# Where kept tiles are sent from, which row sums VectorE adds, and how the last attention ends: one change to a two-layer graph kernel

## The chip, the cores and the metric

The kernel runs on one core of one Trainium2 chip. A core has TensorE (PE: matrix products into PSUM, and loads of the stationary operand, PEld), VectorE (DVE), ScalarE (ACT), GpSimd (POOL) and SyncE (SP), which run side by side, each in the order of its own instruction list, and wait for each other by semaphores. Data between the chip's memory (DRAM below) and the on-chip buffers is moved by DMA engines, to which SP, ACT and POOL hand transfers. The metric is device time of one execution in microseconds (us), lower is better. Everything is computed in 32-bit floats.

## The reference, cut to what matters

Input is x (4096 nodes, 512 features) and a 0/1 adjacency adj (4096 x 4096). Two layers with a residual follow each other. Layer 0 is an auto-encoder with four attention heads that uses one attention twice, layer 1 a usual graph attention with four heads of 128 features:

```python
h = jnp.maximum(_layernorm(x), 0.0)
# layer 0: encoder attention, batch norm, MLP, decoder attention (same att), MLP
Xw  = jnp.einsum('hnd,hde->hne', Xh, W)
sig = jax.nn.sigmoid(f1[:, :, None] + f2[:, None, :])
att = masked_softmax(sig, adj)                       # per head, 4096 x 4096
Xn  = _batchnorm(jnp.einsum('hij,hjd->hid', att, Xw))
emb = _mlp_block(Xn)                                 # elu(x W + b) + x, batch norm
Y   = jnp.einsum('hij,hjd->hid', att, emb)           # then W, elu, _mlp_block
x   = x + out
# layer 1: graph attention
h = jnp.maximum(_layernorm(x), 0.0)
logits = leaky_relu(e_s[:, :, None] + e_n[:, None, :], 0.2) masked by adj
x = x + relu(softmax(logits) @ feats + b)
```

So three large attentions are computed: the encoder's, the decoder's (same weights as the encoder's, other values) and the graph attention's. In each, a weight tile is made from a row of target scores and a column of source scores, masked, and multiplied with the values; the row sums of the weights are the denominators of the softmax.

## The kernel before, in words

All three attentions go through one function, `attention` (L221). It works on eight blocks, four heads times two halves of 2048 targets. A block has 32 steps j, one for each 128 source nodes. A step makes one weight tile `e` (128 x 2048) and then four matmuls of 128 x 512 (L371, and L368 for the fourth bank of the first steps) add its products to four PSUM banks.

- **Encoder** (kept="write"). ScalarE makes tanh (L450) and exp (L451), VectorE multiplies by the mask (L452). The mask of a step is loaded by SP (L210, 256 KB as bytes, five buffers); the target row of the next block is loaded by SP too (L203, 1 MB). Every fifth weight tile (j % 5 == 4) is kept for the decoder: ScalarE's queue stores it to DRAM (`ekeep`, L358, 1 MB), three steps later in the program, and the last of a block in the next block (L412) or, in the last block, at its end (L410). `weight_tile` (L249) hands out eight buffers here.
- **Decoder** (kept="read"). The same, without row sums, and every fifth tile is loaded by SP from `ekeep` (L343).
- **Graph attention.** ScalarE makes a Relu with scale and bias (L905), VectorE adds a column and multiplies by the mask (L906). Nine buffers.

Row sums in encoder and graph attention are collected in three ways, and the plans at L62 to L69 say which step goes which way: "moved" tiles are added up by accumulating DMAs that POOL issues (L386), steps "by ones" go to a PSUM bank `den` by four narrow matmuls with ones (`add_to_den`, L259), and the rest VectorE adds to a tile `acc` (L392, L394). At a block's end `acc` goes through the ones matmuls as well; with a third entry True in the plan (`ends_later`), the sum of the moved tiles follows in step 1 of the next block.

In all blocks but the last, the results stay in SBUF or PSUM and are finished within the next block, by a list of things due at step numbers (`at`, L290, and `ending`, L294): copy out of PSUM, denominators through DRAM, inverse, spread over the partitions, multiplication, and what follows. The last block of graph attention finishes at once (L421 to L442): the last two steps' products are made after the row sums (`late`, L376 and L423), VectorE adds a small number to the sums and inverts them (L434, L435), four matmuls with the identity spread the inverses over the partitions (L440), and per 512 targets ScalarE adds the self term (`out_gat`, L911), VectorE multiplies (L915), ScalarE adds the bias with Relu (L918), VectorE adds the residual (L921) and SP writes the result (L922). The encoder's last block takes the same way with one late step.

The order on each engine is that of a scheduler over the program, with `pinned` and `tc.issue_after` as orders written by hand. Every engine works its list in order, so a store in ScalarE's list that waits for a tile holds up the activations behind it.

Of the kernel before, what the change touches and what calls it, by code (L numbers as in the profile page):

```python
# [31 lines left out]
FP = mybir.dt.float32  # L32
# [39 lines left out]

# [13 lines left out]
def kernel(ctx, tc, x, xT, adjT, w0, w0T, v0, wencT, wdecT, vecs, w1, w1T, a1, outT):  # L86
# [132 lines left out]


    def attention(what, keep, pools, weights, values, row_of, out, finish, ebufs, modes=None, invert=None,  # L221
                  kept=None, sums=None, sums2=None, extras={}, row0=None, masks0=(), in_parts0=1):

# [97 lines left out]
        for n, (h, tb) in enumerate(blocks):  # L321
# [7 lines left out]
            adds, held, stores, next_row = [], [], [], None  # L329
            for j in range(NJ):  # L330

                with pinned(products_of):
# [9 lines left out]
                if store and kept == "read":  # L342
                    a_load = nc.sync.dma_start(e, ekeep[h][tb][j // KEEP])  # L343
                else:
                    if masks0:
                        a, a_load = masks0.pop(0)
                    else:
                        a = mask_tile(keep)
                        a_load = load_mask(a, tb, j)

                    with pinned(products_of[:1] if kept == "read" and n == 0 and j < 8 else []):
                        products_of = weights(e, rowb, a, j, h, SB if NJ * n + j < in_parts0 else 1)
                    if store:
                        stores.append((j // KEEP, e))

                    if j % KEEP == KEEP - 3 and stores:
                        k, t = stores.pop()
                        nc.scalar.dma_start(ekeep[h][tb][k], t)  # L358

                def products():  # L360
                    nonlocal last_main, last_ones
# [11 lines left out]
                    last_ones = None  # L373


                if last and invert is not None and j >= NJ - (1 if kept is not None else 2):  # L376
                    late.append((j, e))
                else:
                    products()
                if j < EVICT:  # L380
                    ahead.append((j, e))
                if invert is not None:
                    if j in moved:

# [36 lines left out]
            for s, b in enumerate(po):  # L421
                for k, t in late:
                    nc.tensor.matmul(b, block(values[h], k), t[:, s * IB:(s + 1) * IB], start=(k == 0),  # L423
                                     stop=(k == NJ - 1))
# [10 lines left out]
            nc.vector.reciprocal(inv, inv)  # L435
            if kept is not None:
                nc.gpsimd.dma_start(rinvs[h][tb].rearrange("o (s i) -> (o s) i", i=IB), inv[0:P:32, :])
            for s, o in enumerate(outs):
                rb = bank()
                nc.tensor.matmul(rb, ident[:, 32 * s:32 * s + 1].to_broadcast([P, P]), inv, start=True, stop=True)  # L440
                for f in finish:
                    f(spool, h, tb, s, o, rb, True)  # L442
# [14 lines left out]
    with tc.tile_pool(name="keep", bufs=1) as keep:  # L457
# [149 lines left out]
        def mlp_block(work, w, src, dst, gamma, beta, scale, between, early=None):  # L607
# [11 lines left out]
            for o in range(C):  # L619
# [7 lines left out]
                for ib in range(NIB):  # L627
# [16 lines left out]
                    nc.vector.bn_stats(stats[:, o, ib, :], d)  # L644
                    between(o, ib)
                bn_coefs(stats, gamma, beta, a_mlp, b_mlp, o, o + 1)
            return last_product

        with tc.tile_pool(name="m_small", bufs=1) as small, tc.tile_pool(name="m_work", bufs=3) as work:
# [7 lines left out]
            mlp_block(work, w, xc, yc, "enc_mlp_bn_gamma", "enc_mlp_bn_beta", a_att, lambda o, ib: None, last_head)  # L657


            for h in range(H):  # L660
# [50 lines left out]
    with tc.tile_pool(name="l_small", bufs=1) as small, tc.tile_pool(name="l_work", bufs=2) as work:  # L711
# [22 lines left out]
                nc.sync.dma_start(outT[o * P:(o + 1) * P, :], x1[o])  # L734
            return added

        def between(o, ib):
# [178 lines left out]

    def add_to_output(spool, h, tb, s, o, rb, last):
        nc.scalar.activation(o, o, AF.Relu, bias=vec_of("b")[:, h:h + 1])  # L918
        dst = nodes(outT[h * P:(h + 1) * P, :], tb * SB + s)
        if last:  # L920
            nc.vector.tensor_add(o, o, x1_last[0][:, s * IB:(s + 1) * IB])  # L921
            nc.sync.dma_start(dst, o)  # L922
        else:
            nc.gpsimd.dma_start(dst, o, accum_op=ALU.add)

    with tc.tile_pool(name="gat", bufs=1) as spool:
        x1_last = []

        def load_last(load):
            x1_last.append(spool.tile([P, TB], FP, name="rowb", bufs=2))  # L930
            nc.sync.dma_start(x1_last[0], outT[(H - 1) * P:H * P, (NTB - 1) * TB:NTB * TB])

        with tc.issue_after(last_pe.ins):
            attention("gat", spool, spool, gat_weights, v1, lambda h, tb: (rowsg, tb * H + h), out_gat,
                      (scaled_gat, add_to_output), 7, lambda n: (GAT_FIRST, *[GAT] * (H * NTB - 2), GAT_LAST)[n],
                      (N * TINY, ALU.add), sums=R[2][:, 0:TB], sums2=(row0, R[2][:, TB:N]), row0=row0, in_parts0=3,
                      extras={(0, 1): rest_of_rows, (H * NTB - 1, NJ - 10): load_last})


def _inputs(x, adj, w):  # L940
# [39 lines left out]
```

## Time and profile before

| what | us |
|---|---|
| median of three runs | 3258.72 |
| runs, lowest to highest | 3256.42 to 3258.72 |
| the profiled execution | 3257.38 |
| its span | 3255.6 |
| stage: first layer norm, projections | 0 to 67 |
| stage: encoder attention | 67 to 1050 |
| stage: encoder MLP, heads | 1050 to 1192 |
| stage: decoder attention | 1192 to 2078 |
| stage: decoder MLP, second layer norm, values | 2078 to 2330 |
| stage: graph attention | 2330 to 3252 |

The profile is of one execution; its span runs from the first to the last recorded instruction, and 1.8 us of the execution lie around it. Times in a view count from the start of the span. A busy total says how long an engine worked, not what set the end; that is read from waits (what released an engine that stood idle) and from windows cut by stage. In a timeline the columns are start, duration, engine, line and operation, tiles, shape and count of instructions in the group, and in square brackets the idle time ahead of the group with what released it. The granted clock of TensorE was 0.998 of full speed in the mean.

The blocks of the encoder begin at about 67, 203, 327, 448, 567, 686, 805 and 923 us; in the trace the first two are longer (136 and 124) than the other six (119 to 121).

### The profile page before, as it was taken

The numbers are of one execution on the slowest core, as the hardware profiler recorded it, in microseconds if no ns is written. First come the engines' busy times: TensorE is split into PE (matmuls) and PEld (weight loads), VectorE is DVE, ScalarE is ACT, GpSimd is POOL, SyncE is SP. The second block draws the span as 40 slices with busy tenths as digits, with TensorE's granted clock in tenths as the row PEclk, the third lists the DMA queues.
The fourth block names the chain that finished last, engine by engine and source line by source line (L and its number), as shares of the span: only waits on it lengthen the run. The fifth ranks groups of instructions, "written<-read, shape, count | busy, mean of one in ns | idle before, by whom it ended". The sixth has DMA issues, their size and how long they took to land.

```text
span 3255.6 us, 26153 instructions
## 1 busy us (share of the span) xinstructions
PE 3197.0 (98%) x8755; PEld 1483.5 (46%) x8755; DVE 2661.1 (82%) x1953; ACT 2597.9 (80%) x1884; POOL 478.7 (15%) x622
## 2 busy tenths in 40 slices
PE   7999999999999999999999999999999999999999
PEld 6334434444444464444444444448644444444443
DVE  7999999999999665556655665585699999999998
ACT  7999999999997459899999999566765666666664
POOL 2001211211211000000000000025412222222221
PEclk9999999999999999999999999999999999999999
DMA  9998988988986023433443443231489999889985
GB/s 210 197 196 229 268 227 224 270 230 220 271 234 162 2 68 132 146 129 133 145 147 120 137 155 121 77 123 58 128 204 219 219 226 241 220 206 236 221 216 142
DMA packets 211153, 578.51 MB, mean 178 GB/s; under 512 B 25069, under 2 KB 28173, under 8 KB 195017
## 3 DMA queue, kind: packets, MB, share of 16 engines
q0 software_dynamic: 67968, 222.51, 36.0%
q1 hardware_dynamic: 126432, 293.72, 26.5%
q10 hardware_dynamic: 16616, 60.60, 4.8%
q8 instruction: 69, 1.13, 0.1%
q14 instruction: 68, 0.55, 0.0%
HBM read 377.10 MB, written 84.29 MB: 142 GB/s over the span
## 4 chain that ended last, share of the span: by engine, by line
PE 67%; DVE 15%; issue 7%; ACT 6%; DMA 5%; POOL 0%; DVEq 0%; ACTq 0%; POOLq 0%
PE ps L371 51%; DVE e L452 9%; PE ps L615 7%; PE ps L811 3%; ACT e L450 3%; DMA a<-mask 3%; DVE acc L394 2%; ACT e L451 2%; DMA acc<-e 1%; PE den L262 1%; DVE R L394 1%; PE ps L672 1%; DVE e L906 1%; PE ps L368 1%; PE ps L537 1%
## 5 line engine op out<-in xcount | busy, mean ns | idle before, releaser
L371 PE MATMUL ps<-e,R 128*128 128x512 f32 x6024 | 2612.8, 594 | 34.8 <-DVE e L452 32.6
L371 PEld LDWEIGHTS ps<-e,R 128*128 128x128 f32 x6024 | 1139.8, 190 | 1500.7 <-issue 1398.1
L452 DVE TENSOR_TENSOR e<-e,a 128x2048 f32<-128x2048 f32 (+1 forms) x470 | 1052.2, 2261 | 391.2 <-ACT e L451 373.5
L450 ACT ACTIVATE e<-rowb,score 128x2048 f32<-128x2048 f32 (+1 forms) x470 | 912.3, 1967 | 86.2 <-PE ps L371 45.6
L451 ACT ACTIVATE e<-e 128x2048 f32<-128x2048 f32 (+1 forms) x470 | 870.5, 1879 | 6.1
L905 ACT ACTIVATE e<-rowb,nq,jcol 128x2048 f32<-128x2048 f32 x224 | 461.9, 2090 | 273.5 <-DMA w<-e 124.9
L906 DVE SCALAR_TENSOR_TENSOR e<-e,jcol,a 128x2048 f32<-128x2048 f32 (+1 forms) x265 | 593.6, 2280 | 7.7 <-ACT e L905 7.7
L394 DVE TENSOR_TENSOR acc<-acc,e 128x2048 f32<-128x2048 f32 x126 | 288.1, 2286 | 2.0
L394 DVE TENSOR_TENSOR R<-R,e 128x2048 f32<-128x2048 f32 x123 | 282.1, 2294 | 0.0
L386 POOL DMA_DIRECT2D w<-e x178 | 150.7, 849 | 612.5 <-DMA w<-e 356.3
L615 PE MATMUL ps<-R,w 128*128 128x512 f32 x512 | 220.3, 592 | 0.7 <-DVE w L573 0.7
L386 POOL DMA_DIRECT2D acc<-e x144 | 120.7, 883 | 536.5 <-DMA acc<-e 193.0
L287 POOL DMA_DIRECT2D rb<-rinvs x60 | 34.6, 582 | 1060.8 <-DVE R L563 867.5
L615 PEld LDWEIGHTS ps<-R,w 128*128 128x128 f32 x512 | 97.2, 190 | 122.7 <-issue 117.9
L636 ACT ACTIVATE ex<-ps,bias 128x512 f32<-128x512 f32 x64 | 44.0, 688 | 98.5 <-PE ps L615 78.7
L811 PE MATMUL ps<-w1x,hT 128*128 128x260 f32 x512 | 115.5, 384 | 1.4 <-ACT hT L789 1.4
L811 PEld LDWEIGHTS ps<-w1x,hT 128*128 128x128 f32 x512 | 96.5, 190 | 19.9 <-issue 3.3
L905 ACT ACTIVATE e<-w,nq,jcol 128x2048 f32<-128x2048 f32 (+1 forms) x41 | 67.4, 1710 | 24.9 <-DMA R<-e 24.9
L638 DVE SCALAR_TENSOR_TENSOR ex<-ex,re 128x512 f32<-128x512 f32 x64 | 45.0, 703 | 36.4 <-ACT re L637 36.2
L848 POOL TENSOR_TENSOR vacc<-vacc,R 128x128 f32<-128x128 f32 x120 | 65.9, 579 | 45.2 <-ACT R L841 44.8
L841 ACT ACTIVATE R<-ps,rstd 128x128 f32<-128x128 f32 x128 | 38.7, 371 | 29.2 <-PE ps L811 25.4
L262 PE MATMUL den<-e,ones 128*32 128x512 f32 x456 | 54.9, 598 | 0.0
(173 smaller groups left out, 1246.5 us busy)
## 6 DMA issues: line engine op xcount, KB each, us to landing
a<-mask SPq DMA_DIRECT2D x720, 256.0 KB, 4.2
w<-e POOLq DMA_DIRECT2D x178, 512.0 KB, 6.7
acc<-e POOLq DMA_DIRECT2D x144, 512.0 KB, 6.7
ekeep<-e ACTq DMA_DIRECT2D x48, 1024.0 KB, 7.8
e<-ekeep SPq DMA_DIRECT2D x48, 1024.0 KB, 4.8
mask<-in_adjT POOLq DMA_DIRECT2D x8, 2048.0 KB, 102.3
rowb<-rows SPq DMA_DIRECT2D x16, 1024.0 KB, 7.0
rb<-rinvs POOLq DMA_DIRECT2D x60, 256.0 KB, 4.0
```

The source lines that it names most:

```text
L262: last_ones = nc.tensor.matmul(den[s * 32:(s + 1) * 32, :], ones[:, 0:32], t[:, s * IB:(s + 1) * IB], start=start, stop=stop)
L371: last_main = nc.tensor.matmul(b, block(values[h], j), e[:, s * IB:(s + 1) * IB], start=(j == 0), stop=(j == NJ - 1))
L386: nc.gpsimd.dma_start(into_half, e_half, **({"accum_op": ALU.add} if j > moved[0] else {}))
L394: nc.vector.tensor_add(acc, acc, e)
L450: nc.scalar.activation(e, rowb, AF.Tanh, bias=column(score[:, 1], j, h), scale=0.5)
L451: last_act = nc.scalar.activation(e, e, AF.Exp, scale=0.5)
L452: last_dve = nc.vector.tensor_mul(e, e, a)
L615: last = nc.tensor.matmul(z, w[:, fb, o * P:(o + 1) * P], nodes(src[fb], ib), start=(fb == 0), stop=(fb == C - 1))
L811: m = nc.tensor.matmul(banks[k][:, 0:2 * DX], hT[:, fb, c * P:(c + 1) * P], w1x[:, fb, 2 * k:2 * k + 2, :].rearrange("p h x -> p (h x)"), ...
L848: nc.gpsimd.tensor_add(vacc[:, h, :], vacc[:, h, :], block(v1[h], j))
L905: last_act = nc.scalar.activation(e, rowb, AF.Relu, bias=column(nq, j, h), scale=column(jcol, j, h))
L906: last_dve = nc.vector.scalar_tensor_tensor(e, e, column(jcol2, j, h), a, ALU.add, ALU.mult)
```

## The change

It has these parts:

- **Stores.** From the third encoder block on, SP stores the kept tiles instead of ScalarE, and the store stands later in the program: at the next storing step, behind that step's mask load. Blocks 0 and 1 stay on ScalarE.
- **Plan of encoder block 1.** Seven moved steps instead of six, other steps by ones; VectorE adds 17 tiles instead of 18.
- **Encoder's last block.** The additions for steps 26 and later are made at the end (`at_end`); the decoder's first two weight tiles' multiplications are ordered behind the batch-norm statistics of the MLP's second column block, first node block (`behind`).
- **Graph attention, blocks 1 to 6.** Step 30 is added by VectorE instead of by ones.
- **Graph attention, last block.** Steps 30 and 31 by ones instead of step 12; four late steps instead of two; the inverses are written to DRAM and read back into all partitions by SP in four parts, and two VectorE operations per 512 targets finish the output (`finish_gat`): (product + self term) x inverse, then the larger of that and −b, added to the residual, to which ScalarE has added b some steps before. L440 and the four-step finish of that block (L911, L915, L918, L921) are gone.

```diff
-ENC_SECOND = (13, 15, 17, 20, 22, 25), (5, 6, 10, 11, 23, 24, 30, 31)
+ENC_SECOND = (12, 14, 17, 19, 22, 24, 26), (1, 2, 4, 5, 7, 8, 30, 31)
-GAT = tuple(range(3, 28, 2)), (30, 31), True
+GAT = tuple(range(3, 28, 2)), (31,), True
-GAT_LAST = (3, 5, 7, 9, 11, 13, 15, 17, 19, 21, 23), (12,)
+GAT_LAST = (3, 5, 7, 9, 11, 13, 15, 17, 19, 21, 23), (30, 31)
...
-                    with pinned(products_of[:1] if kept == "read" and n == 0 and j < 8 else []):
+                    with pinned([*(products_of[:1] if kept == "read" and n == 0 and j < 8 else ()),
+                                 *(behind if n == 0 and j < EP else ())]):
                         products_of = weights(e, rowb, a, j, h, SB if NJ * n + j < in_parts0 else 1)
+                    if stores and (store if n > 1 else j % KEEP == KEEP - 3):
+                        k, t = stores.pop()
+                        (nc.sync if n > 1 else nc.scalar).dma_start(ekeep[h][tb][k], t)
                     if store:
                         stores.append((j // KEEP, e))
-                    if j % KEEP == KEEP - 3 and stores:
-                        k, t = stores.pop()
-                        nc.scalar.dma_start(ekeep[h][tb][k], t)
...
-                if last and invert is not None and j >= NJ - (1 if kept is not None else 2):
+                if last and invert is not None and j >= NJ - (1 if kept is not None else 4):
                     late.append((j, e))
...
-                        if len(adds) == 2:
+                        if last and kept is not None and j >= NJ - 6:
+                            at_end.append(e)
+                        elif len(adds) == 2:
                             nc.vector.tensor_add(acc, *adds)
                         elif len(adds) > 2:
                             nc.vector.tensor_add(acc, acc, e)
+                    if j == NJ - 1:
+                        for t in at_end:
+                            nc.vector.tensor_add(acc, acc, t)
...
             for k, t in stores:
                 if last:
-                    nc.scalar.dma_start(ekeep[h][tb][k], t)
+                    nc.sync.dma_start(ekeep[h][tb][k], t)
                 else:
-                    at(EVICT, nc.scalar.dma_start, ekeep[h][tb][k], t)
+                    at(EVICT, (nc.sync if n > 1 else nc.scalar).dma_start, ekeep[h][tb][k], t)
...
-            outs = [out(spool, h, tb, s, po[s]) for s in range(SB)]
+            outs = [out(spool, h, tb, s, po[s]) for s in range(SB)] if finish_last is None else po
...
+            elif finish_last is not None:
+                nc.sync.dma_start(rinvs[h][tb].rearrange("o (s i) -> (o s) i", i=IB), inv[0:P:32, :])
+                rbs = [rb for rb, in in_parts(SB, acc)]
+                for s, rb in enumerate(rbs):
+                    nc.sync.dma_start(rb, everywhere(rinvs[h][tb], 0, s * IB, IB))
+                for s, rb in enumerate(rbs):
+                    finish_last(h, tb, s, po[s], rb)
+                continue
...
+    def finish_gat(h, tb, s, po, rb):
+        x1b, nb = x1_last
+        o = R[2][:, TB + s * IB:TB + (s + 1) * IB]
+        nc.vector.scalar_tensor_tensor(o, po, ssum[:, h:h + 1], rb, ALU.add, ALU.mult)
+        nc.vector.scalar_tensor_tensor(o, o, nb, x1b[:, s * IB:(s + 1) * IB], ALU.max, ALU.add)
+        nc.sync.dma_start(nodes(outT[h * P:(h + 1) * P, :], tb * SB + s), o)
...
+            x1_last.append(edge.tile([P, 1], FP, name="nb"))
+            nc.vector.tensor_scalar_mul(x1_last[1], vec_of("b")[:, H - 1:H], -1.0)
+        def add_bias(load):
+            nc.scalar.activation(x1_last[0], x1_last[0], AF.Identity, bias=vec_of("b")[:, H - 1:H])
...
+            mlp_block(work, w, xc, yc, "enc_mlp_bn_gamma", "enc_mlp_bn_beta", a_att,
+                      lambda o, ib, made: behind_it.append(made) if (o, ib) == (1, 0) else None, last_head)
...
-                      kept="read", extras={(1, 6): sums_of_weights, (1, 16): bias_of_decoder})
+                      kept="read", behind=behind_it, extras={(1, 6): sums_of_weights, (1, 16): bias_of_decoder})
```

More of the change, by code (lines that the diff above doesn't have):

```diff
@@ L221, in attention @@
     def attention(what, keep, pools, weights, values, row_of, out, finish, ebufs, modes=None, invert=None,
-                  kept=None, sums=None, sums2=None, extras={}, row0=None, masks0=(), in_parts0=1):
+                  kept=None, sums=None, sums2=None, extras={}, row0=None, masks0=(), in_parts0=1,
+                  finish_last=None, behind=()):
         spool, made, masks0 = pools, 0, list(masks0)
@@ L328, in attention @@
             po, ahead, late = [bank() for _ in range(SB - 1)], [], []
-            adds, held, stores, next_row = [], [], [], None
+            adds, held, stores, at_end, next_row = [], [], [], [], None
             for j in range(NJ):
@@ L643, in mlp_block @@
                         nc.vector.scalar_tensor_tensor(d, nodes(src[o], ib), scale[:, o:o + 1], ex, ALU.mult, ALU.add)
-                    nc.vector.bn_stats(stats[:, o, ib, :], d)
-                    between(o, ib)
+                    made = nc.vector.bn_stats(stats[:, o, ib, :], d)
+                    between(o, ib, made)
                 bn_coefs(stats, gamma, beta, a_mlp, b_mlp, o, o + 1)
@@ L655, in last_head @@
                 scale_weights(C - 1)
-            mlp_block(work, w, xc, yc, "enc_mlp_bn_gamma", "enc_mlp_bn_beta", a_att, lambda o, ib: None, last_head)
+            behind_it = []
+            mlp_block(work, w, xc, yc, "enc_mlp_bn_gamma", "enc_mlp_bn_beta", a_att,
+                      lambda o, ib, made: behind_it.append(made) if (o, ib) == (1, 0) else None, last_head)
             for h in range(H):
@@ L735, in residual, with between @@
             return added
-        def between(o, ib):
+        def between(o, ib, made):
             if o in (1, 2):
@@ L918, in add_to_output @@
         nc.scalar.activation(o, o, AF.Relu, bias=vec_of("b")[:, h:h + 1])
[L919 to L924, printed above, removed]
+        nc.gpsimd.dma_start(nodes(outT[h * P:(h + 1) * P, :], tb * SB + s), o, accum_op=ALU.add)
+    def finish_gat(h, tb, s, po, rb):
[4 more added lines that the diff above has]
+        nc.sync.dma_start(nodes(outT[h * P:(h + 1) * P, :], tb * SB + s), o)
     with tc.tile_pool(name="gat", bufs=1) as spool:
@@ L936 @@
                       (N * TINY, ALU.add), sums=R[2][:, 0:TB], sums2=(row0, R[2][:, TB:N]), row0=row0, in_parts0=3,
-                      extras={(0, 1): rest_of_rows, (H * NTB - 1, NJ - 10): load_last})
+                      extras={(0, 1): rest_of_rows, (H * NTB - 1, NJ - 10): load_last, (H * NTB - 1, NJ - 4): add_bias},
+                      finish_last=finish_gat)
 def _inputs(x, adj, w):
```

## The prediction

> **What bounds the kernel now.** I read the busy totals first, then the chain that ended last, then the waits of TensorE, then windows by stage.
>
> ```profile
> PE 3197.0 (98%) x8755; PEld 1483.5 (46%) x8755; DVE 2661.1 (82%) x1953; ACT 2597.9 (80%) x1884; POOL 478.7 (15%) x622
> ...
> PE 67%; DVE 15%; issue 7%; ACT 6%; DMA 5%; POOL 0%; DVEq 0%; ACTq 0%; POOLq 0%
> ```
>
> ```profile
> PE ps L371 <- DVE e L452: 32.6, 25, 3.9
> ```
>
> TensorE is busy 98% of the 3255.6 us span, so only two things can pay: its 59 us of idle time, or fewer matmuls. Of the idle time, 32.6 us is waits for the mask multiply L452, nearly all in the encoder's attention (67 to 1050). Decoder and MLPs are TensorE-bound and start when the encoder ends, so what the encoder saves arrives at the end one for one. The windows tell the stages apart (length, then busy PE, PEld, DVE, ACT, POOL, granted clock, DMA share, GB/s):
>
> ```profile
> 74.70:80.20 5.50, 5.40 (x8) 2.03 (x8) 4.53 (x3) 5.50 (x4) 0.00 (x0) 0.69 1.05 159
> 567.00:686.00 119.00, 116.47 (x309) 49.83 (x306) 114.87 (x64) 118.87 (x65) 22.61 (x31) 1.00 0.88 239
> 2902.00:3016.00 114.00, 114.00 (x292) 49.31 (x288) 110.38 (x54) 71.77 (x42) 25.61 (x30) 1.00 0.93 221
> ```
>
> An encoder block (second row) belongs to **ScalarE**: 118.87 of 119 us, TensorE 2.53 idle. A graph-attention block (third) belongs to **TensorE**: no idle, VectorE with 3.6 us to spare.
>
> **Part 1: kept tiles on SyncE from block 2 on.** ScalarE's timeline shows what a store costs there:
>
> ```profile
> 590.32 1.89 ACT L451 ACTIVATE e<-e 128x2048 f32<-128x2048 f32 x1
> 590.67 0.33 ACTq L358 DMA_DIRECT2D ekeep<-e  x1
> 592.11 1.89 ACT L451 ACTIVATE e<-e 128x2048 f32<-128x2048 f32 x1
> 593.91 1.99 ACT L450 ACTIVATE e<-rowb,score 128x2048 f32<-128x2048 f32 x1
> 595.93 1.91 ACT L451 ACTIVATE e<-e 128x2048 f32<-128x2048 f32 x1
> 597.75 1.99 ACT L450 ACTIVATE e<-rowb,score 128x2048 f32<-128x2048 f32 x1
> ```
>
> The issue (0.33) lies under a running activation. But where a store sits between tanh and exp, the schedule drops the pairing "two tanh, two exp": a lone pair takes 597.75 − 593.91 = 3.84 us, a step within pairs 7.39 / 2 = 3.695. The instruction order shows four such steps per block turned into pairs: 4 × 0.145 = **0.58 us per block**, in a ScalarE-bound stage. The Trainium skill ("DMA: Bandwidth & Descriptors", "Issuing engines are not separate DMA queues") speaks against the move: DMAs of all issuers run on the same 16 engines and interleave, and another issuer saves only the sequencer's issue time. By that, 36 stores × 0.33 = 11.9 us if issue time were exposed; by the row nothing for the issue and 0.58 × 6 = 3.5 for the pairing. I take the row.
>
> On SP a store stands behind a mask load that waits for the same multiply, so it adds no new wait; each 1 MB store now stands ahead of the next masks, though. A mask has five buffers: 5 × 3.7 − 2.2 = 16.3 us from issue to need. Stores of blocks 2 to 7 landed after 3.8 to 9.3 us (median 7.5), masks after 2.4 to 9.4 (4.6). The nearest row is the next block's 1 MB row, already on SP: issued at 617.33, landed after 9.46 us, and VectorE waited for no mask from 460 to 1045. Price nothing; other end in the rivals.
>
> **Part 2: block 1's new plan** (six to seven tiles moved, other tiles summed by ones, three VectorE additions fewer by step 10).
>
> ```profile
> 218.41 0.35 ACTq L358 DMA_DIRECT2D ekeep<-e  x1
> 218.81 3.90 ACT L450 ACTIVATE e<-rowb,score 128x2048 f32<-128x2048 f32 x2 [4.61 <-DVE e L452]
> ```
>
> ScalarE reached the first store at 214.2 and stood 4.61 us, since VectorE multiplied tile 4 only by 218.4: it ran some 12 us behind. With fewer additions ahead of it that multiply ends at 202.1 + copies 2.5 + two multiplies 4.4 + 0.6 + one addition 2.2 + multiply 2.2 = 214.0, so the stall goes. A second stall of 3.95 us (274.86: a tanh waits for the buffer of moved tile 15, whose accumulating DMAs landed at 274.76) goes too, since the moves start one step earlier and have some 10 us of margin. ScalarE gains 8.56. TensorE's idle time caps what arrives: 3.73 us in block 1 (1.64 + 0.80 + 1.29) and 4.45 in block 2 (1.63 + 0.19 + 0.83 + 1.80), together 8.2; what is left of ScalarE's gain falls due in blocks 3 to 6. By the end of block 2 ScalarE is 8.56 + 0.58 = 9.1 ahead, by block 6 9.1 + 4 × 0.58 = **11.5**; TensorE still has 2.53 idle per block, so it follows.
>
> **Part 3: the encoder's end.** TensorE waits 0.49 (1026.67) and 1.80 us (1035.60) there for late multiplies, because VectorE makes additions (2.2 each) and the decoder's first masks before tiles 30 and 31. After the change four additions come behind them (one between) and the decoder's multiplies behind an MLP operation with slack on VectorE (six tenths busy in that slice of the page). Both waits go: **−2.3**. The additions end near 1037.4, the sums are needed near 1039.1: 1.7 us of cover; without it the excess shows. The waits 0.57 (dsb) and 0.65 (MLP weights) stay. Encoder: −11.5 − 2.3 = **−13.8**.
>
> **Part 4: graph attention, one step less by ones in blocks 1 to 6.** A step by ones is four matmuls, 0.87 us between the starts of the row "den" and the next (3236.69, 3237.57). Six are gone: −5.2 on TensorE. VectorE gets an addition of 2.2 in each: 110.3 → 112.5 against TensorE's 113.97 − 0.87 = 113.1. It stays ahead, by 0.6 us a block, so no wait within these blocks.
>
> **Part 5: the end.**
>
> ```profile
> 3236.69 1.06 PE L262 MATMUL den<-w,ones 128*32 128x512 f32 x8
> 3237.57 1.04 PE L262 MATMUL den<-R,ones 128*32 128x512 f32 x8
> 3238.54 7.13 PE L423 MATMUL ps<-e,R 128*128 128x512 f32 x16
> 3245.51 3.60 PE L440 MATMUL ps<-dsb,ident 128*128 128x512 f32 x8
> ```
>
> ```profile
> 3239.41 3.35 DVE L435 RECIPROCAL dsb<-dsb 128x512 f32<-128x512 f32 x1
> ...
> 3251.75 0.69 DVE L921 TENSOR_TENSOR R<-R,rowb 128x512 f32<-128x512 f32 x1 [0.19 <-ACT R L918]
> ```
>
> Before: late products until 3245.5, a broadcast by TensorE (L440), then 12 short ScalarE and VectorE steps to 3252.44. After: VectorE was level with TensorE at 2441.2 (a wait of 0.76 in the first block). From there its work is 110.2 + 5 × 112.5 + 117 (last block: 32 × 2.265 + 19 × 2.2 + 2.75), so multiply 31 ends near 3230.9, while TensorE's tile 27 ends at 3236.7 − 6.9 − 1.0 − 5.2 = 3223.6. **A new wait**: about 2.4 us for the ones of tile 30, 2.7 for those of 31. The sums are complete near 3233.5; L434 (0.69) and the reciprocal (3.35) end at 3237.7. The inverses go through DRAM: no such pair is here; nearest rows are the write in the quiet after the encoder (1.78 us) and the read into 128 partitions after the decoder (3.53), the dear end is 4.2 + 9.1 as seen in the busy attention. At the end masks and moves are over, so I take the quiet ones: first part at 3243.2, fourth near 3245. Fifteen late products (0.43 each) end near 3246.4; two VectorE steps follow the last: 3247.9. **−4.5**; with the dear end 3237.7 + 13.3 + 4 × 0.7 = 3253.8: +1.4.
>
> A rule speaks against this end: by the Trainium skill ("TensorE: Matmul & The Clock Gate", "Part 1: The HAM clock gate") an idle window of some 3.4 us halves TensorE's clock for about 3.4 us. The trace agrees at 74.72: after a wait of 3.90 us the granted clock is 0.69 for 5.5 us, and eight matmuls took 5.4 instead of 3.43. After waits of 1.80 and 2.12 the products ran at full pace. The new waits of 2.4 and 2.7 are parted by matmuls; by the row next to them they cost nothing, by the rule taken as one window 3.4 / 2 = +1.7. I take nothing and keep 1.7.
>
> **Sum.** −13.8 − 4.5 = −18.3 from the profiled execution's 3257.4: **3239 us**. (The median shown is 1.3 higher, its lowest run 1.0 lower.)
>
> **Rivals.**
> - *Block 1 stalls elsewhere.* ScalarE waits at its next store or buffer instead: only 3.5 − 0.6 + 2.3 of the encoder's gain and 4.5 at the end: 3247. For: POOL's queue in block 1 is held up by the mask casts (an 8 KB move issued at 214.68 landed at 239.93). Against: 10 us of margin. 14%.
> - *The end gives its gain back* (dear DRAM hop, cold clock, or VectorE later than summed): 3257.4 − 13.8 + 0 to 1.4 = 3244 to 3245. 20%.
> - *Slower: stores hold up masks in SP's queue.* If the queue serves strictly in order and a store takes S, the mask behind lands at S + 2.4 at the earliest and VectorE waits once S passes 13.9. At S = 16 that is 2.1 × 6 stores − 3.9 (VectorE's idle per block) = 8.7 per block, 52 in six: 3291; break-even at S = 15.1. For: in block 0 (DMA share 1.05) the row took 20.6 us and VectorE waited for masks. Against: 11.2 is the slowest store. 3%.
> - *It doesn't do what it says*: VectorE, not TensorE, bounds graph attention, its waits spread over all blocks and the six additions (13.2) show: 3257.4 − 13.8 + 8 = 3252. Against: 3.6 us idle per block. 5%.
>
> The forecast has 58%. A measurement of this kernel tells about 0.2% (6.5 us) from no change. Faster by more 90%, within it 6%, slower 4%. The range takes in both DRAM ends, the clock, block 1's stalls, and below 3239 a further 2.5 each from last waits and the end: 3231 to 3251.
>
> **What would show it.** Right: ScalarE's 4.61 and 3.95 gone, encoder blocks near 118.2, graph blocks 113.1, two waits of 2 to 3 us before the last sums, last write near 3234 on the new scale. Wrong: VectorE waiting for masks in the encoder, waits of TensorE inside graph blocks 1 to 6, or a clock below 1 in the last 10 us.

## The result, and the profile after

| | before | changed |
|---|---|---|
| median of eight runs, us | 3257.93 | 3247.59 |
| lowest to highest | 3255.26 to 3258.72 | 3246.14 to 3249.32 |
| span of the profiled execution | 3255.6 | 3247.1 |

The ratio is 0.997, its 95% interval 0.9959 to 0.998: 10.3 us less where 18.3 were summed. Between the two profiled executions it is 8.5. Line numbers shift by the change: mask multiply L452 is L472 after it, tanh L450 is L470, exp L451 is L471, products L371 are L376, late products L423 are L434, additions L394 are L401 and, deferred, L405, graph attention's L905 and L906 are L928 and L929.

The page and the waits of the changed kernel, for the lines shown of before:

```profile
PE 3193.9 (98%) x8707; PEld 1482.1 (46%) x8707; DVE 2667.0 (82%) x1958; ACT 2586.3 (80%) x1877; POOL 477.2 (15%) x624
...
PE 67%; DVE 17%; issue 7%; DMA 6%; ACT 3%; DVEq 0%; POOL 0%; ACTq 0%; POOLq 0%; SPq 0%
```

```profile
PE ps L376 <- DVE e L472: 24.6, 22, 3.9
```

The totals have hardly moved; TensorE's waits for the mask multiply fell by 8.0 us. Windows of the stages (length, busy PE, PEld, DVE, ACT, POOL, granted clock, DMA share, GB/s), an encoder block and a graph-attention block:

```profile
559.00:677.00 118.00, 116.37 (x305) 49.31 (x304) 114.15 (x64) 118.00 (x65) 22.35 (x29) 1.00 0.89 241
...
2902.00:3016.00 114.00, 114.00 (x283) 49.43 (x282) 114.00 (x57) 70.51 (x41) 25.23 (x30) 1.00 0.95 224
```

In the second row VectorE is now as full as TensorE. The added addition takes 2.3 of its 3.6 us, and the shorter block (112.4 us of VectorE's work in place of 114.0) the rest. Where the time went is told best by the end of VectorE's mask multiply of step 31 in each encoder block, and by three later marks (all read from the two traces, in us; differences are of unrounded times):

| mark | before | changed | difference | change of the difference |
|---|---|---|---|---|
| block 0 | 195.17 | 194.88 | −0.29 | −0.29 |
| block 1 | 318.64 | 317.02 | −1.62 | −1.33 |
| block 2 | 439.85 | 437.95 | −1.89 | −0.27 |
| block 3 | 558.59 | 558.22 | −0.37 | +1.52 |
| block 4 | 677.34 | 676.40 | −0.93 | −0.56 |
| block 5 | 796.11 | 794.58 | −1.53 | −0.60 |
| block 6 | 914.87 | 912.76 | −2.10 | −0.57 |
| start of the MLP's first products | 1050.61 | 1044.81 | −5.80 | −3.70 |
| step 31, first block of graph attention | 2441.22 | 2435.41 | −5.81 | −0.01 |
| last VectorE operation | 3252.44 | 3243.75 | −8.69 | −2.88 |

Blocks 4 to 6 gain the 0.58 of the sum, the encoder's end gains more than was summed, and graph attention 2.9 of 4.5. The large miss is in blocks 1 to 3: most of the 8.6 us that the forecast took from ScalarE's waits should have come through there, and next to nothing did.

**What took it in block 1.** VectorE's timeline of the changed kernel:

```profile
216.67 2.29 DVE L472 TENSOR_TENSOR e<-e,a 128x2048 f32<-128x2048 f32 x1 [0.63 <-DMA a<-mask]
221.68 2.29 DVE L472 TENSOR_TENSOR e<-e,a 128x2048 f32<-128x2048 f32 x1 [2.71 <-DMA a<-mask]
...
229.59 2.29 DVE L472 TENSOR_TENSOR e<-e,a 128x2048 f32<-128x2048 f32 x1 [1.17 <-DMA a<-mask]
```

```profile
DVE e L472 <- DMA a<-mask: 6.8, 5, 2.7
```

VectorE comes earlier to its multiplies and stands for masks, 6.8 us from 200 to 320 us (second fence) instead of 1.8. In the trace the last of the eight transfers that turn the adjacency into byte masks lands at 241.8 us (239.2 before), and the three mask loads between 203 and 245 us whose landing is recorded took 13.8 to 17.8 us (4.4 to 13.3 before); from 245 to 320 the median was 5.7. That the transfers into byte masks are what slows these loads is read from the times alone; no kernel without them was made. Before, ScalarE's stall of 4.61 us kept VectorE behind these loads; with the old plan of the block back (run b) VectorE stands 1.8 us for masks again. ScalarE's waits from 200 to 320 us fell from 9.4 us to 3.1 (L265 are the ones matmuls that read a tile before its buffer comes free):

```profile
ACT e L471 <- DVE e L472: 1.8, 2, 1.3
ACT e L470 <- PE den L265: 1.3, 2, 1.0
```

**What took the rest in block 2.** ScalarE's timeline, and POOL's beside it:

```profile
358.51 1.99 ACT L470 ACTIVATE e<-rowb,score 128x2048 f32<-128x2048 f32 x1
362.50 2.00 ACT L470 ACTIVATE e<-rowb,score 128x2048 f32<-128x2048 f32 x1 [2.01 <-DMA acc<-e]
...
393.76 2.00 ACT L470 ACTIVATE e<-rowb,score 128x2048 f32<-128x2048 f32 x1 [1.60 <-DMA acc<-e]
...
403.62 2.01 ACT L470 ACTIVATE e<-rowb,score 128x2048 f32<-128x2048 f32 x1 [2.36 <-DMA acc<-e]
```

```profile
332.01 0.90 POOL L272 DMA_DIRECT2D dens<-dsb  x1
342.53 0.57 POOL L277 DMA_DIRECT2D dcol<-dens  x1 [9.62 <-DMA dens<-dsb]
343.09 1.82 POOL L391 DMA_DIRECT2D acc<-e  x2
350.39 0.84 POOL L391 DMA_DIRECT2D acc<-e  x1 [5.48 <-DMA acc<-e]
353.18 0.86 POOL L391 DMA_DIRECT2D acc<-e  x1 [1.95 <-DMA acc<-e]
353.72 0.88 POOL L285 DMA_DIRECT2D rinvs<-dcol  x1
362.89 1.63 POOL L290 DMA_DIRECT2D rb<-rinvs  x3 [8.29 <-DMA rinvs<-dcol]
364.49 1.85 POOL L391 DMA_DIRECT2D acc<-e  x2
```

A tanh waits for the buffer of a moved tile (of tiles 7, 15 and 17 in the three waits shown), whose accumulation is late: POOL works its list in order, stands 9.62 us for the denominators' way through DRAM and 8.29 for the inverses', and each accumulation waits for the one before it (5.48, 1.95). Tile 7 was ready at 342.0; its second half landed at 362.4, and at that moment the tanh begins. In the trace before, the same half landed at 363.8, the halves behind the two other waits at 394.6 and 404.0 (393.7 and 403.5 after): the chain was as late, but ScalarE, delayed by block 1, came just in time for it: no wait of it stands between 320 and 440 us. In the changed kernel it waits 7.3 us there (6.2 for accumulations, 1.1 for sums by ones), more than the 6.3 that it gained in block 1.

### The profile page after: what moved, and what is told of

Read it like the earlier page. It is cut to its first block, busy times and chain, and to the rows that moved or that the text cites. A ratio compares the mean times of both kernels' runs of the same rounds, so it can differ in the third digit from the quotient of the medians.

```text
span 3247.1 us, 26119 instructions
## 1 busy us (share of the span) xinstructions
PE 3193.9 (98%) x8707; PEld 1482.1 (46%) x8707; DVE 2667.0 (82%) x1958; ACT 2586.3 (80%) x1877; POOL 477.2 (15%) x624
## 4 chain that ended last, share of the span: by engine, by line
PE 67%; DVE 17%; issue 7%; DMA 6%; ACT 3%; DVEq 0%; POOL 0%; ACTq 0%; POOLq 0%; SPq 0%
PE ps L376 51%; PE ps L635 7%; DVE e L472 4%; DMA a<-mask 4%; DVE R L401 4%; DVE acc L401 4%; DVE e L929 4%; PE ps L834 3%; PE den L265 2%; ACT e L470 1%; PE ps L373 1%; PE ps L695 1%; ACT e L471 1%; DMA w<-e 1%; PE ps L557 1%
## 5 line engine op out<-in xcount | busy, mean ns | idle before, releaser
L376 PE MATMUL ps<-e,R 128*128 128x512 f32 x6008 | 2607.1, 594 | 27.1 <-DVE e L472 24.6
L376 PEld LDWEIGHTS ps<-e,R 128*128 128x128 f32 x6008 | 1137.5, 190 | 1489.4 <-issue 1391.2
L472 DVE TENSOR_TENSOR e<-e,a 128x2048 f32<-128x2048 f32 (+1 forms) x470 | 1052.8, 2259 | 394.7 <-ACT e L471 371.7
L470 ACT ACTIVATE e<-rowb,score 128x2048 f32<-128x2048 f32 (+1 forms) x470 | 912.3, 1970 | 83.8 <-PE ps L376 45.5
L471 ACT ACTIVATE e<-e 128x2048 f32<-128x2048 f32 (+1 forms) x470 | 869.6, 1880 | 7.1 <-DVE e L472 1.8
L928 ACT ACTIVATE e<-rowb,nq,jcol 128x2048 f32<-128x2048 f32 x224 | 459.1, 2088 | 263.4 <-DMA w<-e 148.4
L929 DVE SCALAR_TENSOR_TENSOR e<-e,jcol,a 128x2048 f32<-128x2048 f32 (+1 forms) x265 | 593.6, 2276 | 2.8 <-ACT e L928 2.8
L401 DVE TENSOR_TENSOR R<-R,e 128x2048 f32<-128x2048 f32 x128 | 293.1, 2290 | 0.0
L401 DVE TENSOR_TENSOR acc<-acc,e 128x2048 f32<-128x2048 f32 x121 | 276.3, 2283 | 0.9
L928 ACT ACTIVATE e<-w,nq,jcol 128x2048 f32<-128x2048 f32 (+1 forms) x41 | 67.4, 1713 | 26.0 <-DMA R<-e 26.0
L265 PE MATMUL den<-e,ones 128*32 128x512 f32 x416 | 50.8, 599 | 4.7 <-DVE e L929 4.7
```

The lines of the kernel that those rows point to most:

```text
L265: last_ones = nc.tensor.matmul(den[s * 32:(s + 1) * 32, :], ones[:, 0:32], t[:, s * IB:(s + 1) * IB], start=start, stop=stop)
L376: last_main = nc.tensor.matmul(b, block(values[h], j), e[:, s * IB:(s + 1) * IB], start=(j == 0), stop=(j == NJ - 1))
L470: nc.scalar.activation(e, rowb, AF.Tanh, bias=column(score[:, 1], j, h), scale=0.5)
L471: last_act = nc.scalar.activation(e, e, AF.Exp, scale=0.5)
L472: last_dve = nc.vector.tensor_mul(e, e, a)
L928: last_act = nc.scalar.activation(e, rowb, AF.Relu, bias=column(nq, j, h), scale=column(jcol, j, h))
```

## The experiments

All medians below are of five rounds or more, beside runs of the kernel before on the same chip; these had medians of 3258.75 (runs a, b, c, f), 3258.53 (d, e, g, h), 3257.53 (i, j, k) and 3257.56 (l). From one profiled execution to the next the end of block 0 fell between 193.3 and 200.7 us, so a gain in a stage is read from marks within one trace. Differences of medians are against the 3247.59 of the changed kernel, in another series; the kernel before moved by 1.2 us from series to series, so a difference of that size tells nothing by itself.

### a and k: all stores by ScalarE

Run a, the old place:

```diff
-                    if stores and (store if n > 1 else j % KEEP == KEEP - 3):
-                        k, t = stores.pop()
-                        (nc.sync if n > 1 else nc.scalar).dma_start(ekeep[h][tb][k], t)
                     if store:
                         stores.append((j // KEEP, e))
+                    if stores and j % KEEP == KEEP - 3:
+                        k, t = stores.pop()
+                        nc.scalar.dma_start(ekeep[h][tb][k], t)
```

> The changed kernel with all stores of kept tiles back on ScalarE, at their old place; all else as changed. Theory 1 (the encoder's missing gain was lost to limits of blocks 1 and 2 that have nothing to do with the stores' queue: masks behind the casts' traffic until 240 us, then the chain of accumulating DMAs): the waits of ScalarE for accumulating DMAs in block 2 stay at about 6 us; blocks 3 to 6 lose the pairing, 118.2 to 118.75 each; +2.5 to +3.5 us against the changed kernel, 3250 to 3251. Rival (1 MB stores in SP's queue crowd masks and accumulations, and that is where the gain went): the waits in block 2 go, the encoder ends some 5 us sooner, 3243 to 3245.

Measured: 3258.24 us (ratio to before 0.9998, 0.9989 to 1.0006). Without the stores' move the whole change gains nothing: in the traces the MLP begins 3.7 us later than in the kernel before, and graph attention is 4.4 us shorter. The waits for accumulations stay (7.7 us in block 2, 6.2 in the changed kernel) and blocks 4 to 6 take 118.75, as theory 1 has it, so the rival, crowding in SP's queue, falls. Stores land after 6.9 us (median from 440 to 1045) on SP, 7.3 on ScalarE before, masks after 4.8 and 4.5. The cost, though, is three times what theory 1 said. Against the changed kernel's trace block 2 lost 4.4 us, blocks 4 to 6 1.7, and from block 6 to the MLP's start 3.7: TensorE's waits of 0.49 and 1.80 before the last multiplies are there again, although the deferral of the additions is in this kernel. In its instruction order VectorE makes two additions between multiplies 29 and 30, as before. Why block 2 lost as much as 4.4 us stays open.

Run k, the new place in the program, but ScalarE's list:

```diff
-                        (nc.sync if n > 1 else nc.scalar).dma_start(ekeep[h][tb][k], t)
+                        nc.scalar.dma_start(ekeep[h][tb][k], t)
```

(the two stores at a block's end likewise)

> The changed kernel with all stores by ScalarE, but at the new, later place in the program. Theory 2 (it is the store in ScalarE's own list that parts the pairs and so turns VectorE's order): blocks 3 to 6 take 118.75 us, TensorE's waits of 0.5 to 1.8 us at the end of the last block stay, +8 to +11 us as with the old place, 3255.5 to 3258.6. Rival (the later place is what matters): within 1.5 us of the changed kernel, 3246 to 3249.

Measured: 3260.34 us (1.0006, 0.9998 to 1.0014). The later place is not what matters; the list it stands in is. TensorE's waits at the end of the encoder's last block were 1.80 and 0.83, and block 4 took 119.8, block 5 118.75, block 6 119.4, and the time is above the range expected, with single waits of ScalarE for accumulations (1.72 at 516 us, 0.57 at 754) that run a doesn't have.

### j: the stores' move alone, on the kernel before

The diff is that of part 1, and nothing else.

> The kernel before with part 1 alone: stores of kept tiles by SP from the third encoder block on. Theory 2 (parts 1 and 3 need each other: with whole pairs on ScalarE the scheduler also orders VectorE anew, and in the last block puts additions and the decoder's first multiplications ahead of the copies out of PSUM): encoder blocks 3 to 6 take 118.2 us, but TensorE waits near 4.8 us at the start of the MLP: +0 to +2.5 against the kernel before, 3258 to 3261. The sum as predicted (the pairing is worth 3.5 us by itself): 3254.5.

Measured: 3259.44 us (1.0008, 1.0 to 1.0016). Blocks 4 to 6 take 118.2, and all of it is given back at the encoder's end, in one wait of 4.77 us. So part 1 alone gains nothing, and the other parts without part 1 gain nothing in sum either (runs a and k).

### c: the encoder's end as before

```diff
-                        if last and kept is not None and j >= NJ - 6:
+                        if last and kept is not None and j >= NJ:
...
-                      kept="read", behind=behind_it, extras=...
+                      kept="read", extras=...
```

> The changed kernel with the encoder's last additions in their old places and the decoder's first multiplications where the scheduler puts them. If the last block's gain is these two waits of TensorE (0.49 and 1.80): both are back, +2.3 to +3.1 us, 3250 to 3250.7. Rival (the last block gains by the pairing alone): within 0.6 us, no wait of TensorE before the last products.

Measured: 3255.09 us (0.9988, 0.9981 to 0.9996), +7.5. The two waits that the sum was about are not the ones that come back. TensorE's and VectorE's timelines of run c:

```profile
1037.23 3.70 PE L434 MATMUL ps<-e,R 128*128 128x512 f32 x8
1045.70 5.34 PE L460 MATMUL ps<-dsb,ident 128*128 128x512 f32 x8 [4.77 <-DVE dsb L446]
```

```profile
1029.88 2.29 DVE L401 TENSOR_TENSOR acc<-acc,e 128x2048 f32<-128x2048 f32 x1
1032.09 6.90 DVE L472 TENSOR_TENSOR e<-e,a 128x2048 f32<-128x2048 f32 x6
1038.90 1.91 DVE L579 COPY R<-ps 128x512 f32<-128x512 f32 x3
...
1041.58 0.68 DVE L445 TENSOR_SCALAR dsb<-den 128x512 f32<-128x512 f32 x1
1042.29 3.35 DVE L446 RECIPROCAL dsb<-dsb 128x512 f32<-128x512 f32 x1
```

The six multiplies at 1032.09 are the encoder's last and the decoder's first (four parts and a whole one, 4.6 us); behind them the scheduler puts the copies out of PSUM, and only then the inverse, for which TensorE's broadcast L460 waits 4.77 us. The wait of 4.77 us stands at the same place in run j. So once ScalarE's pairs are whole the scheduler orders VectorE anew, and parts 1 and 3 belong together.

### b and l: the old plan of encoder block 1

```diff
-ENC_SECOND = (12, 14, 17, 19, 22, 24, 26), (1, 2, 4, 5, 7, 8, 30, 31)
+ENC_SECOND = (13, 15, 17, 20, 22, 25), (5, 6, 10, 11, 23, 24, 30, 31)
```

> The changed kernel with the old plan of encoder block 1. Theory 1 (what the new plan takes off ScalarE's stalls is waited for again, for masks in block 1 and for accumulations in block 2): the stalls of 4.6 and 4.0 us are back in block 1, the waits of ScalarE for accumulations in block 2 fall from 6 us to under 2, and the time is 0 to 2 us above the changed kernel: 3247.6 to 3249.6. The sum as predicted (the plan's gain arrives at the end): +8 us, 3256.

Measured: 3248.73 us (0.9971, 0.996 to 0.9983), +1.1. The stalls are back (4.58 and 3.97 us), and ScalarE's wait for accumulations in block 2 is one of 1.43 us instead of 6: what isn't waited for in block 1 is waited for in block 2. From the end of block 0 to that of block 3 the two kernels differ by 0.25 us.

### f: a shorter chain in encoder block 2

```diff
+ENC_THIRD = (0, 2, 5, 10, 12, 15, 20, 22, 25), (7, 8, 9, 30, 31)
...
-                          (scaled, statistics), 6, lambda n: (ENC_FIRST, ENC_SECOND, ENC)[min(n, 2)],
+                          (scaled, statistics), 6, lambda n: (ENC_FIRST, ENC_SECOND, ENC_THIRD, ENC)[min(n, 3)],
```

> The changed kernel with another plan for encoder block 2 alone: steps 7 and 17 are not moved any more (7 by ones, 17 added by VectorE), nine moved instead of eleven. Theory 1 (the chain of accumulating DMAs on POOL's queue bounds block 2 and holds ScalarE 6 us): those waits fall under 1.5 us, block 2 takes 118 to 119 us instead of 121, and block 3 loses nothing to a late ScalarE: -3 to -4.5 us, 3243 to 3244.5. Rival (DMA traffic at large bounds block 2, so that other transfers are late instead): ScalarE or VectorE waits as long for others, within 1 us of 3247.6. If VectorE, with one addition more, becomes the bound of block 2: +1.

Measured: 3242.28 us (0.9947, 0.9933 to 0.996), −5.3. ScalarE's waits from 320 to 440 us, first the changed kernel, then run f (engine and line, what it waited for: us, times, longest):

```profile
ACT e L470 <- DMA acc<-e: 6.2, 4, 2.4
```

```profile
ACT e L471 <- PE den L266: 2.1, 2, 1.1
```

No tanh waits for an accumulation any more. From the end of block 0 to that of block 3 the trace is 5.1 us shorter (358.2 against 363.3): two steps of eleven taken off POOL's chain let the gain of block 1 through. The rival, traffic at large, falls: no other wait took the place of these. Two of the three tiles waited for (7 and 17) are not moved any more in run f, so their waits would go in any case; tile 15 still is, and its accumulation lands at 387.8 instead of 393.7. So the chain is shown, but not each of its links; a kernel with the denominators on another queue wasn't tried.

Run l is run i (below), which has this plan, with the old plan of block 1:

> The kernel with the thinner block 2 and two more ones at the end (3240.6), with the old plan of encoder block 1. Theory 1 (the new plan's gain was eaten by the accumulations of block 2; with these out of the way it arrives): ScalarE loses the difference of its waits in block 1, 9.4 before against 4.2 us as changed: +3 to +4.5 us, 3243.6 to 3245.1. Rival (block 1 itself took it, by late masks): under +1.5, below 3242.1.

Measured: 3244.98 us (0.9959, 0.9946 to 0.9973), +4.4 against run i (in another series; the kernel before had 3257.56 and 3257.53 in the two). In the traces blocks 1 to 3 take 361.8 us against 358.0. So part 2 is worth about 1 us in the kernel as changed, no more than the series differ, and some 4 with block 2 out of the way. Late masks took only a part.

### d, e, g, h: graph attention

Run d takes part 4 back, run e part 5 (plan, two late steps, the spread by TensorE), run g sums two more steps of the last block by ones, run h has two late steps instead of four:

Run d:

```diff
-GAT = tuple(range(3, 28, 2)), (31,), True
+GAT = tuple(range(3, 28, 2)), (30, 31), True
```

Run e (with it the last block's bias and residual as before, L917 to L922):

```diff
-GAT_LAST = (3, 5, 7, 9, 11, 13, 15, 17, 19, 21, 23), (30, 31)
+GAT_LAST = (3, 5, 7, 9, 11, 13, 15, 17, 19, 21, 23), (12,)
-                if last and invert is not None and j >= NJ - (1 if kept is not None else 4):
+                if last and invert is not None and j >= NJ - (1 if kept is not None else 2):
...
-                      finish_last=finish_gat)
```

Run g:

```diff
-GAT_LAST = (3, 5, 7, 9, 11, 13, 15, 17, 19, 21, 23), (30, 31)
+GAT_LAST = (3, 5, 7, 9, 11, 13, 15, 17, 19, 21, 23), (12, 18, 30, 31)
```

Run h:

```diff
-                if last and invert is not None and j >= NJ - (1 if kept is not None else 4):
+                if last and invert is not None and j >= NJ - (1 if kept is not None else 2):
```

> The changed kernel with step 30 summed by ones again in graph-attention blocks 1 to 6. Theory G (from the third block on VectorE, not TensorE, sets the pace up to the last tile; the 5.2 us taken from TensorE came back as its two waits of 2.34 us at the end): TensorE's last block ends 5 us later, the two waits go, the sums are complete at the same time and the end is within 0.7 us of the changed kernel, 3247 to 3248.3. As predicted (part 4 is worth 5.2 less the waits that part 5 makes): +0.5 at most. If part 4 is worth its 5.2 in full: 3252.8.

> The changed kernel with the old end of the last block: its plan (step 12 by ones), two late steps, the inverses spread by TensorE, the finish by ScalarE and VectorE; blocks 1 to 6 as changed. Theory G (the new end starts its sums no sooner, and has twice the products, 13.5 us, behind them): VectorE's last multiply some 2 us sooner, two additions behind it, last VectorE operation about 3241.6 on the changed kernel's scale, 2 us sooner: 3245 to 3246. Rival (the spread by TensorE and the four-step finish cost more than the DRAM hop): +1 to +4 us, 3248.5 to 3251.5.

> The changed kernel with steps 12 and 18 of the last graph-attention block by ones too, so two additions of 2.2 us less on VectorE and 1.74 us more on TensorE there. Theory G: multiply 31 ends 4.4 us sooner, TensorE's two waits fall from 4.7 us to under 1, sums, inverse and products all move up: -3 to -4.2 us, 3243.4 to 3244.6. Rival (the DRAM hop or the late products set the end, whatever VectorE does): within 1 us, 3246.6 to 3248.6.

> The changed kernel with two late steps in the last graph-attention block instead of four. If the chain sums, inverse, DRAM hop, eight VectorE operations sets the end: the products of steps 28 and 29 fill TensorE's two waits, TensorE ends 6.9 us sooner, the end stays within 0.5 us, 3247 to 3248. If the late products set it: -2 to -6 us, 3241.5 to 3245.5. If the four were needed to let the sums go first: +2 to +3.

| | median, us | first block's step 31 to the last VectorE operation |
|---|---|---|
| before | 3258 | 811.2 (810.9 in run j) |
| changed | 3247.6 | 808.3 (806.9 to 808.5 in six traces with this stage: a, b, c, f and k beside it) |
| d | 3247.7 | 807.3 |
| e | 3246.0 | 805.9 |
| g | 3245.8 | 803.8 (and in runs i and l) |
| h | 3247.8 | 807.6 |

The same stage differs by 1.6 us from trace to trace, so d and h can't be told from the changed kernel; e is 0.9 to 2.6 shorter than its six traces. Against 811.2 before, part 5 without part 4 (d) gains 3.9, part 4 without part 5 (e) 5.3, as summed (5.2), and both together 2.7 to 4.4. So on top of the other each gains nothing, and the two don't add. VectorE tells why: from 2450 to 3220 us it was busy 757.65 of 770 us before, and 770 in the changed kernel. It had 12.4 us to give, and six additions of 2.2 take 13.2.

g is 3.1 to 4.7 shorter by the stage, about what theory G (VectorE sets the pace of graph attention, in the expectation of run d) summed. By the medians it is 1.8 (run i against run f: 1.7), and its interval (0.9945 to 0.997 of before) overlaps the changed kernel's; that difference stays open. The late products don't set the end (h): without two of their four steps TensorE is done 7.7 us before the last VectorE operation, and the stage is as long. TensorE's last stretch in the changed kernel, and then in run g:

```profile
3220.07 1.07 PE L265 MATMUL den<-e,ones 128*32 128x512 f32 x8 [2.34 <-DVE e L929]
3221.07 1.13 PE L434 MATMUL ps<-e,R 128*128 128x512 f32 x2
3224.54 1.07 PE L265 MATMUL den<-e,ones 128*32 128x512 f32 x8 [2.34 <-DVE e L929]
3225.42 1.48 PE L265 MATMUL den<-w,ones 128*32 128x512 f32 x8
3226.66 1.95 PE L265 MATMUL den<-R,ones 128*32 128x512 f32 x8
3228.54 13.51 PE L434 MATMUL ps<-e,R 128*128 128x512 f32 x30
```

```profile
3221.46 1.92 PE L265 MATMUL den<-e,ones 128*32 128x512 f32 x16
3223.20 1.04 PE L265 MATMUL den<-w,ones 128*32 128x512 f32 x8
3224.06 1.04 PE L265 MATMUL den<-R,ones 128*32 128x512 f32 x8
3225.03 14.00 PE L434 MATMUL ps<-e,R 128*128 128x512 f32 x32
```

The two waits are there, 2.34 us each where 2.4 and 2.7 were summed, and in g they are gone, with two additions less on VectorE. Behind the second wait the sums of w and R take 1.48 and 1.95 instead of 1.04 each. Windows of the changed kernel, with the granted clock as the third figure from the right:

```profile
3224.50:3226.50 2.00, 1.96 (x16) 0.58 (x20) 0.00 (x0) 0.00 (x0) 0.00 (x0) 0.85 0.00 0
3226.50:3229.00 2.50, 2.50 (x13) 0.67 (x6) 0.26 (x1) 0.00 (x0) 0.00 (x0) 0.50 0.00 0
```

The clock was halved for some 3.4 us (the matmuls that begin from 3225.85 to 3228.54 last 1.02 to 1.06 us, before and after 0.59).

### i: the two faster ones together

f and g in one kernel.

> The changed kernel with both versions that were faster: nine moved steps in encoder block 2, and steps 12 and 18 of the last graph-attention block by ones too. The two gains lie in stages that do not meet (5.3 us by the median in the encoder, 1.8 by the median and 4.5 by the stage in graph attention), so they add: -7 to -9.8 us, 3238 to 3240.6. Rival (one of them was scatter of the first stage): -5 or less, 3242 and above.

Measured: 3240.62 us (0.9946, 0.9934 to 0.9959 of before), 7.0 below the changed kernel: the fastest of all. The sum of the two gains by the medians was 7.1.

## Why the prediction was right or wrong

- **Total.** Forecast 3239, measured 3247.6, within the range, which was drawn wide enough for block 1's stalls. The sum itself was 8 us too much; in the traces the encoder gave 5.8 of its 13.8 and graph attention 2.9 of its 4.5. The mechanism that ate most of the gain was among the rivals, as "block 1 stalls elsewhere", with 14%, too little. That its 3247 is so near is in part luck, since it had the end's 4.5 in full. It looked for ScalarE's next store or buffer in block 1; the runs show late masks there, and the buffers of moved tiles in the block after.
- **Part 1, 0.58 per block.** Right: blocks 4 to 6 gain 0.56 to 0.60. That stores in SP's queue would cost nothing was right too; the slower rival found no footing. What was missed is that the scheduler turns VectorE's order with ScalarE's. Alone the part is worth nothing (j), and without it the others are worth nothing in sum (a, k). Summing parts one by one assumed that they are independent.
- **Part 2, the step that failed.** "ScalarE gains 8.56" and "TensorE still has 2.53 idle per block, so it follows" asked only who works, not what the next buffer or mask waits for. Both signs stood in the first profile: denominators issued at 214.68 that landed at 239.93, just behind the last transfer into byte masks (239.2), and accumulations in block 2 landing when ScalarE needs the buffer. The 10 us of margin was worked out for the stall in block 1 and not asked for in block 2. Measured: ScalarE gained 6.3 us in block 1 (waits of 9.4, then 3.1) and lost 7.3 in block 2 (none, then 7.3).
- **Part 3.** −2.3 summed; with its share of pairing −2.9, the stage gave −3.7. Both waits are gone. What the part is worth beside part 1 is 7.5 (c), since it also keeps the decoder's multiplies from in front of the inverse.
- **Part 4.** Right as to the blocks: VectorE takes 112.4 us for one and TensorE 113.1, without a wait of TensorE within the blocks, and the 5.2 us were there at tile 27. Nearly all of it came back as the two waits of 2.34 that part 5's list named. "VectorE with 3.6 us to spare" held for blocks 5 and 6 alone: blocks 1 to 3 took it 110.2 us each before, without a pause, and from 2450 to 3220 us it had 12.4 to spare in all.
- **Parts 4 and 5 together, −4.5, measured −2.9** (−2.7 to −4.4 over the six traces). On the scale of the stage multiply 31 ended at 789.1 (789.7 forecast). Two terms were off. The sums came 1.0 late (793.3 for 792.3) by the halved clock: the forecast took the row beside it (no loss after 2.12 us). The rule of the Trainium skill ("TensorE: Matmul & The Clock Gate", "Part 1: The HAM clock gate", an idle window of some 3.4 us, then half the clock) gave 1.7 when the two waits were taken as one window, and that was nearer to the 1.4 measured. As it stands it asks for a longer wait than either of 2.34, so the measurement decides. And after the first part of the inverses (802.6, forecast 802.0, so the quiet DRAM rows were right) eight VectorE operations of 0.72 follow each other; the forecast had let two of them follow the last product. The products were right: "0.43 each" is one of the two records of a matmul, but their forecast end (3246.4, 805.2 on this scale) is reached with 0.86, and they ended at 806.6, late mostly because the sums were. The two ends lie 1.7 us apart, and run h shows that the products alone don't decide.

## What to carry to other kernels

When a stall goes, look up when everything that the freed engine needs next will land (masks, buffers of tiles that another queue still reads), at the new, earlier time: a stall can cover the next one. A change of one engine's list can turn another's order where a scheduler decides, so compare the order on every engine, and don't add up parts that were sized alone. Work moved from the fullest engine to the next fullest pays only until the second is full at the point that sets the end.

## What the runs showed of the hardware that was not expected

Waits of TensorE of about 2 us halve its clock at times. Of the six profiles with such a pair of waits at the end, the clock fell behind the first in three (runs a, f, k: 0.50 to 0.56 in the 1.6 us after it), behind the second in the changed kernel, behind both in part in run c (0.70 and 0.50), and not at all in run b, with waits of 2.31 and 2.35. Where it falls behind the first, the slower matmuls only fill the second wait (0.77 us in run f) and cost nothing; behind the second they delay the sums by 1.4 us. The stage agrees: 806.9 to 807.1 in a, b, f and k, 808.3 and 808.5 in the changed kernel and c. In the encoder waits of 1.80 and 2.12 showed no such loss before the change, but one of 1.90 in the changed kernel did, from 0.5 us after TensorE had resumed:

```profile
535.66 12.69 PE L376 MATMUL ps<-e,R 128*128 128x512 f32 x25 [1.90 <-DVE e L472]
```

```profile
536.19:539.60 3.41, 3.41 (x6) 1.35 (x5) 3.41 (x3) 3.41 (x3) 1.45 (x2) 0.50 0.93 203
```

At 966.27 the clock fell with no wait before it, behind matmuls of 0.25 us. So the length of the wait alone doesn't tell whether the clock falls; what else it takes, these runs don't show.
